# A two-layer attention hybrid on one core: the matmuls of its main part written as four 128x32 column tiles

## The chip, the cores and the metric

The kernel runs on one core of one Trainium2 chip. The metric is the time of one execution on the device, in microseconds (us). The kernel before took 1532.03 us in the median of three runs (1530.29 to 1536.46). A core has five engines with their own instruction queues: TensorE (PE, matmuls; PEld is its weight load), VectorE (DVE), ScalarE (ACT), GpSimd (POOL) and SyncE (SP), which issues the DMA transfers here.

## The reference: what is computed

The input x has two batches of 2048 tokens with 128 features, in float32. Four residual steps follow one another, each on a layer norm of x:

```
x = x + attn_a(layernorm(x))     # scores x x^T over all 2048 tokens, softmax over the first token axis
x = x + ffn(layernorm(x))        # two layers, below
x = x + attn_b(layernorm(x))     # token weights, channel weights, projection
x = x + ffn(layernorm(x))        # the same two layers once more
```

One layer of `ffn` shifts half of the features by one token, projects to queries, keys and values of 8 heads with 64 features, normalises queries and keys, turns them by a rotary table, attends within windows of 64 tokens and the window before, and projects back; then comes a gated feed-forward part:

```
q, k, v = split(shift(x) @ wqkv);  q, k = rotary(l2norm(q) * qs, l2norm(k) * ks)
x = x + local_attention(q, k, v) @ wo
h = layernorm(shift(x)) @ w1 + b1;  a, g = split(h)
x = x + (a * gelu(g)) @ w2 + b2
```

`attn_b` makes from projected queries and keys one number for each token, sends it through two short convolutions and a softmax over tokens, and multiplies the values by it and by a weight for each channel. All matmuls are in float32 but one small one for the mask.

## The kernel before

**Layout.** The state is held transposed, features on the 128 partitions, tokens along the free axis, in chunks of 512 tokens (`CH`) and blocks of 128 (`P`): 16 blocks for each batch. Matmul results go to eight PSUM banks of 128x512 (`pp` in the profile, kind `p1` in the code).

**A program written by a planner.** The functions do not issue instructions. Each calls `op(engine, cost, fn, r=..., w=..., at=..., mode=...)`, which notes an operation with its reads, writes, an assumed cost and a name. At the end `Program.run` plays all of them through a list scheduler and issues them in the order that comes out. Each operation has a place in line: its number in program order plus the offset for its name in the table `PLACES`. At each moment an engine that is free takes the ready operation with the smallest place. On TensorE `MODE` is added to the place if the operation needs another tiling of the array than the last one; on ScalarE `HOLD` is added if it needs another function table. Buffers are given out in the same pass. So the assumed costs, `PLACES`, `MODE` and `HOLD` set the order on every queue, and nothing else does: each queue then runs in that order, waiting on semaphores.

**Tilings.** TensorE's array of 128x128 can be split. `MODES = "fpsv"` are the four that the kernel before uses: `f`, the whole array; `p`, four column tiles of 128x32; `s`, 64x32 tiles, for the scores of the local attention; `v`, two column tiles of 128x64. The planner's table `SWITCH` has an assumed price for each change.

**Stages.** `first_norm` and `first_attention` do `attn_a` for the first batch (until about 130 us). The second batch's `attn_a` (`second_attention`) is done in slices beside the beginning of the main part. The main part runs 16 blocks x 2 layers x 2 batches x 2 repeats = 128 times through `Attention.block`, 32 times through `feed_forward`, and twice through `token_weights`.

**One block** on TensorE, with the lines of the profile:

- the query and key projections (L663), two operations of eight 128x32 column tiles with 256 columns each, already `p`;
- the value projection (L670), one 128x512 matmul, `f`;
- the sums for the l2 norm (L692), 128x128 by 32 columns, `f`;
- the scores (L733) with the mask added by a bfloat16 matmul (L742), 64x32 tiles, `s`;
- after exp on ScalarE, a scaling on GpSimd, a 32x32 transpose on VectorE and a round trip through DRAM buffers named `far`: the combine (L805), 16 matmuls of 128x64 with 64 columns, `v`;
- for each second block the output projection (L818), four accumulated matmuls of 128x128 by 256 columns, `f`.

`feed_forward` has six matmuls of 128 x (128, 128, 85) by 512 columns (L858) and three accumulated ones of 512 columns (L883), `f`; the means of the norms are L572 (`f`) and L553 (`p`). `second_attention` has L532 and L542 (`f`), `token_weights` L951, L1061, L1063 and some small ones (`f`). The profile shows each float32 matmul as two records of PE and two of PEld.

## Time and profile before

| | before |
|---|---|
| median of 3 runs | 1532.03 us |
| the profiled execution | 1532.57 us, its span 1530.7 us |
| mean granted TensorE clock | 0.968 |
| PE busy | 1409.7 us, 92%, 20867 matmul records |
| PEld busy | 813.8 us, 20867 records |
| DVE, ACT, POOL busy | 1219.0, 1016.3, 1070.7 us |
| chain that ended last | PE 46%, DVE 23%, DMA 10%, POOL 9%, issue 5% |
| DMA | 228.57 MB, of it 2.69 MB in the instruction queue q8 |

How to read it. The page has the busy time of each engine, then the span in 40 equal slices with a digit for the busy tenths (PEclk is the clock that TensorE was granted, in tenths). A line of a group has the line of the kernel, engine, operation, tile names as out<-in, rows*columns of the array, the moving operand, the number of records, then busy us, mean ns of one, and the idle time before with what ended it. A line of the timeline has start and length in us, then the same, with the idle time before in brackets. "issue" means that the engine waited for nothing that the profile shows. Ends of matmuls are modelled, and they overlap; the distance from the start of one operation to that of the next is the better measure.

### The profile page before, as it was taken

Reading aid. Unit: us, or ns where it says so; the run is one execution under the profiler, and the core shown is the slowest. Engines: PE = TensorE matmul, PEld = TensorE weight load, DVE = VectorE, ACT = ScalarE, POOL = GpSimd, SP = SyncE. Lnnn points to the kernel's source line nnn. Section 1 sums busy time; section 2 is a strip of 40 time slices with the busy share of each in tenths; the row PEclk is TensorE's granted clock in tenths of the full one; section 3 lists DMA queues with packets and bytes.
Section 4 is the critical chain, followed back from the end, with each engine's and each line's share of the span. In section 5 each row is a group of like instructions: output and inputs, shape, how many; then the busy total and the mean of one; then the engine's idle time right before and its main releaser. Section 6 shows DMA issues by size and latency. Waiting matters only on the chain.

```text
span 1530.7 us, 52656 instructions
## 1 busy us (share of the span) xinstructions
PE 1409.7 (92%) x20867; PEld 813.8 (53%) x20867; DVE 1219.0 (80%) x2344; ACT 1016.3 (66%) x3503; POOL 1070.7 (70%) x1308
## 2 busy tenths in 40 slices
PE   7999999999999989799999998999999998989865
PEld 4455555554555555555556554555555554655443
DVE  5366766978898989879898899689698979887761
ACT  7345675667767767657787767658576768586651
POOL 3445544857797968659797878469698869786560
PEclk9999999999999999979999999889999999999987
DMA  6441342554656554545656545535656674756441
GB/s 221 160 158 60 102 129 72 151 146 115 171 155 178 169 162 119 149 129 150 203 165 182 157 138 153 151 115 155 194 141 173 170 208 119 217 155 195 133 114 38
DMA packets 213177, 228.57 MB, mean 149 GB/s; under 512 B 40714, under 2 KB 166340, under 8 KB 212932
## 3 DMA queue, kind: packets, MB, share of 16 engines
q1 hardware_dynamic: 212932, 225.22, 51.6%
q8 instruction: 164, 2.69, 0.7%
q14 instruction: 81, 0.66, 0.1%
HBM read 126.46 MB, written 61.98 MB: 123 GB/s over the span
## 4 chain that ended last, share of the span: by engine, by line
PE 46%; DVE 23%; DMA 10%; POOL 9%; issue 5%; ACT 4%; SPq 2%; POOLq 0%; DVEq 0%; ACTq 0%
PE pp L858 7%; PE pp L663 6%; PE pp L883 4%; PE pp L805 4%; PE pp L532 4%; PE pp L516 4%; PE pp L733 3%; DVE b_n L691 3%; DMA b_c<-line 3%; DVE arena L688 3%; PE pp L542 3%; DVE arena L687 3%; PE pp L818 3%; PE pp L508 2%; PE pp L670 2%
## 5 line engine op out<-in xcount | busy, mean ns | idle before, releaser
L663 PE MATMUL pp<-wqkv,b_s 128*32 128x256 f32 x4096 | 255.3, 386 | 8.2 <-POOL b_s L609 4.6
L759 ACT ACTIVATE arena<-pp,b_m 128x96 f32<-128x96 f32 x584 | 190.3, 362 | 49.9 <-DVE b_m L754 46.5
L858 PE MATMUL pp<-b_c,w 128*128 128x512 f32 (+1 forms) x384 | 189.8, 638 | 24.5 <-POOL b_c L854 21.2
L663 PEld LDWEIGHTS pp<-wqkv,b_s 128*32 128x32 f32 x4096 | 122.5, 110 | 116.6 <-issue 27.3
L769 POOL TENSOR_TENSOR arena<-arena,b_m 128x384 f32<-128x384 f32 x146 | 118.1, 826 | 82.3 <-DVE b_m L764 72.0
L759 ACT ACTIVATE right<-pp,b_m 128x96 f32<-128x96 f32 x440 | 143.7, 366 | 37.0 <-DVE b_m L754 30.0
L701 POOL TENSOR_TENSOR arena<-arena,b_n 128x1024 f32<-128x1024 f32 x84 | 160.6, 1914 | 3.1
L733 PE MATMUL pp<-kring,b_c 64*32 64x96 f32 (+1 forms) x8448 | 132.7, 250 | 18.4 <-DVE b_c L710 11.1
L733 PEld LDWEIGHTS pp<-kring,b_c 64*32 64x32 f32 x8448 | 105.6, 107 | 73.4 <-issue 19.9
L695 POOL TENSOR_TENSOR arena<-arena 128x1024 f32<-128x1024 f32 x52 | 123.2, 2370 | 25.6 <-DVE arena L688 21.1
L754 DVE TENSOR_REDUCE b_m<-pp 128x4 f32<-128x384 f32 x256 | 130.1, 541 | 12.8 <-PE pp L742 11.7
L670 PE MATMUL pp<-wqkv,b_s 128*128 128x512 f32 x256 | 138.4, 631 | 0.0
L759 ACT ACTIVATION_READ_ACCUMULATOR arena<-pp,b_m 128x1 f32 x584 | 133.0, 229 | 0.0
L858 PEld LDWEIGHTS pp<-b_c,w 128*128 128x128 f32 (+1 forms) x384 | 68.5, 189 | 112.8 <-issue 68.1
L686 ACT ACTIVATE arena<-pp 128x512 f32<-128x512 f32 x164 | 98.1, 623 | 43.6 <-PE pp L663 40.0
L687 DVE TENSOR_TENSOR arena<-pp,b_tab 128x512 f32<-128x512 f32 x168 | 110.0, 674 | 6.9 <-ACT arena L686 3.8
L769 POOL TENSOR_TENSOR right<-right,b_m 128x384 f32<-128x384 f32 x110 | 89.1, 827 | 32.2 <-DVE b_m L764 30.3
L805 PEld LDWEIGHTS pp<-arena,b_v 128*64 128x64 f32 x2624 | 85.2, 140 | 45.0 <-issue 22.8
L805 PE MATMUL pp<-arena,b_v 128*64 128x64 f32 x2624 | 96.1, 227 | 13.1 <-DVE b_m L754 3.0
L688 DVE TENSOR_TENSOR arena<-pp,b_tab 128x512 f32<-128x512 f32 x160 | 105.0, 673 | 0.3
L759 ACT ACTIVATION_READ_ACCUMULATOR right<-pp,b_m 128x1 f32 x440 | 101.5, 233 | 0.0
L691 DVE TENSOR_REDUCE b_n<-arena 128x32 f32<-128x1024 f32 x82 | 97.7, 1194 | 0.0
(230 smaller groups left out, 3362.1 us busy)
## 6 DMA issues: line engine op xcount, KB each, us to landing
arena<-far SPq DMA_DIRECT2D x82, 512.0 KB
b_tab<-turn SPq DMA_DIRECT2D x128, 256.0 KB
b_v<-b_v SPq DMA_DIRECT2D x248, 128.0 KB
far<-arena SPq DMA_DIRECT2D x324, 96.0 KB
right<-far SPq DMA_DIRECT2D x46, 512.0 KB
far<-right SPq DMA_DIRECT2D x188, 96.0 KB
b_c<-line SPq DMA_DIRECT2D x56, 256.0 KB
turn<-b_tab SPq DMA_DIRECT2D x32, 256.0 KB
```

The costliest lines, as they stand in the source:

```text
L663: pe_.matmul(out=pq[k]()[c * 32 : c * 32 + 32, a * 256 : (a + 1) * 256], lhsT=s()[:, at : at + 32], rhs=wqkv[:, l, c * 256 : (c + 1) * 256 ...
L670: op("PE", 0.865, lambda: pe_.matmul(out=pv(), lhsT=h(), rhs=wqkv[:, l, 2 * INNER : 3 * INNER], start=True, stop=True), r=keys_of(s, q) + ...
L687: op("DVE", dve(512), lambda part3=part3, src=src, trig=trig: dv.tensor_tensor(part3(t1), src(), trig(0), ALU.mult), r=[pq[k], tab], w=[(t ...
L688: op("DVE", dve(512), lambda part3=part3, src=src, trig=trig: dv.tensor_tensor(part3(t2), src(), trig(1), ALU.mult), r=[pq[k], tab], w=[(t ...
L691: op("DVE", dve(1024), lambda: dv.tensor_reduce(nv()[:, 0:32], sq().rearrange("p (h d) -> p h d", d=32), AX.X, ALU.add), r=[sq], w=[nv], a ...
L701: lambda: po_.tensor_tensor(t1().rearrange("p (h d) -> p h d", d=32), t1().rearrange("p (h d) -> p h d", d=32), nr()[:, 0:32].unsqueeze(2) ...
L733: pe_.matmul(out=sim[par]()[a * 32 : a * 32 + 32, pair * 96 + c0 : pair * 96 + c0 + n], lhsT=qT()[rows, pair * P + a * 32 : pair * P + a * ...
L754: op("DVE", dve(384), lambda sim3=sim3, mx=mx: dv.tensor_reduce(mx(), sim3(), AX.X, ALU.max, negate=True), r=[sim[par]], w=[(nm, par)], at ...
L759: ac.activation(p()[:, hd * 96 : (hd + 1) * 96], sim[par]()[:, k * 96 : (k + 1) * 96], AF.Exp, bias=nm()[:, hd : hd + 1], accum_out=rs()[: ...
L769: lambda hs=hs: po_.tensor_tensor(p3()[:, hs, :], p3()[:, hs, :], rs()[:, hs].unsqueeze(2).to_broadcast([P, 4, 96]), ALU.mult),
L805: pe_.matmul(out=av()[par * 64 : par * 64 + 64, pair * P + w * WIN : pair * P + (w + 1) * WIN].rearrange("p (a c) -> p a c", a=2), lhsT=(v ...
L858: op("PE", pe(512), lambda: pe_.matmul(out=p_()[0:n, :], lhsT=w1[:, l, off + j * P : off + j * P + n], rhs=d(), start=True, stop=True), r= ...
```

## The change

A helper `wide(out, *parts)` writes a matmul of up to 128x128 by n columns as column tiles: the columns in pieces of 256, for each accumulated part, for each 32 rows of the output, one 128x32 matmul at `tile_position=(0, m)`. A 128x128 by 512 matmul becomes eight. All matmuls in `second_attention`, `center`, `Attention.block`, `feed_forward` and `token_weights` that used the whole array go through it and are marked `mode="p"`. The combine is written out in the same way: 32 matmuls of 128x32 with 64 columns in place of 16 of 128x64; `v` is then used by nothing. The transposes, `first_attention` and `fold_norm` stay in `f`, the scores in `s`. What is computed stays the same.

Besides, `PLACES` has new offsets throughout, `MODE` goes from 10 to 15 and `HOLD` from 20 to 50, and three assumed costs of the planner are changed; these alter the order of issue and no instruction.

```diff
 PLACES = {
-    "spread1": -71, "spread2": -145, "root1": -93, "root2": -180, "scale1": 39, "scale2": -66, "scale3": -885,
+    "spread1": -693, "spread2": -189, "root1": -243, "root2": -97, "scale1": -197, "scale2": 43, "scale3": -1790,
...
-    MODE = 10
-    HOLD = 20
+    MODE = 15
+    HOLD = 50
...
+    def wide(out, *parts, start=True, stop=True):
+
+        rows, cols = out.shape[0], out.shape[-1]
+        for c in range(0, cols, 256):
+            for k, (lhsT, rhs) in enumerate(parts):
+                for m in range(0, rows, 32):
+                    to, of = slice(m, min(m + 32, rows)), slice(c, min(c + 256, cols))
+                    pe_.matmul(
+                        out=out[to, of], lhsT=lhsT[:, to], rhs=rhs[:, of], start=start and k == 0, stop=stop and k == len(parts) - 1,
+                        tile_position=(0, m),
+                    )
...
-                for m in both:
-                    pe_.matmul(out=acc(), lhsT=xs[m](), rhs=e[m, j](), start=(m == both[0]), stop=(m == both[1]))
+                wide(acc(), *((xs[m](), e[m, j]()) for m in both))
...
-        op("ACT", act(128) + 0.1, lambda: ac.activation(r(), src(), AF.Ln, bias=eps), r=reads, w=[r], act="E", at="root1")
+        op("ACT", act(128) + 0.15, lambda: ac.activation(r(), src(), AF.Ln, bias=eps), r=reads, w=[r], act="E", at="root1")
...
-            op("PE", 0.865, lambda: pe_.matmul(out=pv(), lhsT=h(), rhs=wqkv[:, l, 2 * INNER : 3 * INNER], start=True, stop=True), r=keys_of(s, q) + [wqkv_], w=[pv], claim=[v], at="block3")
+            op("PE", 0.865, lambda: wide(pv(), (h(), wqkv[:, l, 2 * INNER : 3 * INNER])), r=keys_of(s, q) + [wqkv_], w=[pv], claim=[v], mode="p", at="block3")
...
-            op("PE", 0.15, lambda: pe_.matmul(out=pn()[:, 0:32], lhsT=twin, rhs=nv()[:, 0:32], start=True, stop=True), r=[nv, twin_], w=[pn], at="block12")
+            op("PE", 0.15, lambda: wide(pn()[:, 0:32], (twin, nv()[:, 0:32])), r=[nv, twin_], w=[pn], mode="p", at="block12")
...
-                        for par in range(2):
-                            hd, at = 2 * pair + par, (par * 4 + pair) * 32
+                        for c in range(4):
+                            hd, at = 2 * pair + c // 2, (c // 2 * 4 + pair) * 32
                             pe_.matmul(
-                                out=av()[par * 64 : par * 64 + 64, pair * P + w * WIN : pair * P + (w + 1) * WIN].rearrange("p (a c) -> p a c", a=2),
-                                lhsT=(v if w else v0)()[:, hd * DH : (hd + 1) * DH],
-                                rhs=pT().rearrange("p (a c) -> p a c", a=4)[:, 2 * w : 2 * w + 2, at : at + 32], start=True, stop=True,
+                                out=av()[c * 32 : c * 32 + 32, pair * P + w * WIN : pair * P + (w + 1) * WIN].rearrange("p (a c) -> p a c", a=2),
+                                lhsT=(v if w else v0)()[:, hd * DH + c % 2 * 32 : hd * DH + c % 2 * 32 + 32],
+                                rhs=pT().rearrange("p (a c) -> p a c", a=4)[:, 2 * w : 2 * w + 2, at : at + 32], start=True, stop=True, tile_position=(0, c * 32),
                             )
-            op("PE", 0.946, combine, mode="v", r=[pT, v, v0], w=[av], claim=[oT], at="block30")
+            op("PE", 0.94, combine, mode="p", r=[pT, v, v0], w=[av], claim=[oT], at="block30")
...
-                    for k in range(4):
-                        pe_.matmul(out=po()[:, 0:256], lhsT=wo[:, l, k, :], rhs=oT()[:, k * 256 : (k + 1) * 256], start=(k == 0), stop=(k == 3))
+                    wide(po()[:, 0:256], *((wo[:, l, k, :], oT()[:, k * 256 : (k + 1) * 256]) for k in range(4)))
...
-            op("PE", pe(512), lambda: pe_.matmul(out=p_()[0:n, :], lhsT=w1[:, l, off + j * P : off + j * P + n], rhs=d(), start=True, stop=True), r=[d, w1_], w=[p_], claim=h, at="half1")
+            op("PE", pe(512), lambda: wide(p_()[0:n, :], (w1[:, l, off + j * P : off + j * P + n], d())), r=[d, w1_], w=[p_], claim=h, mode="p", at="half1")
...
-            for j, n in enumerate(HSZ):
-                pe_.matmul(out=po(), lhsT=w2[0:n, l, j, :], rhs=h[j]()[0:n, :], start=(j == 0), stop=(j == 2))
+            wide(po(), *((w2[0:n, l, j, :], h[j]()[0:n, :]) for j, n in enumerate(HSZ)))
```

## The prediction

> **What bounds the kernel now.** I read the page first (span, busy rows, chain), then the groups of TensorE by form, then windows by stage, and last the timeline of TensorE alone, start to start.
>
> From the page of the kernel before:
>
> ```profile
> span 1530.7 us, 52656 instructions
> PE 1409.7 (92%) x20867; PEld 813.8 (53%) x20867; DVE 1219.0 (80%) x2344; ACT 1016.3 (66%) x3503; POOL 1070.7 (70%) x1308
> PEclk9999999999999999979999999889999999999987
> q8 instruction: 164, 2.69, 0.7%
> PE 46%; DVE 23%; DMA 10%; POOL 9%; issue 5%; ACT 4%; SPq 2%; POOLq 0%; DVEq 0%; ACTq 0%
> ```
>
> TensorE (PE) is the fullest engine and carries 46% of the chain; VectorE (DVE) carries 23%. The q8 row matters below: its 2.69 MB over 2 x 20867 matmuls and weight loads are 64 bytes each, and over 164 packets 16 KB each. So q8 carries TensorE's own instructions, 256 to a packet.
>
> Windows of the main part (columns: busy us and counts of PE, PEld, DVE, ACT, POOL, then clock, DMA share, GB/s):
>
> ```profile
> 130.00:330.00 200.00, 200.00 (x2479) 106.89 (x2472) 151.37 (x296) 131.70 (x462) 114.80 (x139) 1.00 0.41 114
> 330.00:1460.00 1130.00, 1048.22 (x17455) 619.18 (x17454) 981.41 (x1853) 791.32 (x2790) 876.97 (x1062) 0.97 0.57 159
> ```
>
> Up to 330 us TensorE never rests: what it saves there is saved. After that DVE is at 87% and PE at 93%, so only a part passes on.
>
> The timeline of TensorE, with a change of tiling at 706.16 and 707.24:
>
> ```profile
> 705.12 1.10 PE L670 MATMUL pp<-wqkv,b_s 128*128 128x512 f32 x2
> 706.16 1.15 PE L805 MATMUL pp<-arena,b_v 128*64 128x64 f32 x32
> 707.24 1.93 PE L663 MATMUL pp<-wqkv,b_s 128*32 128x256 f32 x32
> ```
>
> Start to start, at clock 1.00, over all operations, the common values are: a 512-column whole-array operation followed by another 0.858 us, with its successor's weights exposed 0.942 to 0.963, followed by another tiling 0.952; the column-tiled L663 0.863 (0.887 with weights exposed), 0.977 before another tiling; the 128x64 L805 0.982 and 1.082; the scores (L733 with L742) 0.879 and 1.036. Leaving a tiling thus costs 0.094 (whole), 0.114 (column), 0.100 (128x64), 0.157 (scores). Adding up distances, the 1500 us of operations are 1248 of streaming, 38 extra where the records grant half the clock (they know 1.0 and 0.5), about 90 of switches and exposed weights, 124 of waits.
>
> **The change, part by part.** Terms are TensorE time.
>
> Switches. The order has 641 changes of tiling: 239 leave whole, 173 column, 115 128x64, 114 scores: 239 x 0.094 + 173 x 0.114 + 115 x 0.100 + 114 x 0.157 = 71.6 us. In the same order after the change only the scores and a few transposes differ: 114 x (0.114 + 0.157) + 28 x 0.1 = 33.7. Saving 38.
>
> Exposed weights. Of 562 whole-after-whole operations 189 show the extra 0.084 to 0.104, together 20 us. Column tiles show 0.024, so 4.7 stay: saving 15.
>
> Streaming. Two rounds of four 256-column tiles are what L663 does: 0.863 against 0.858, on some 600 operations, +3. The norm matmul (L692, 32 columns, 128 times) takes 0.140; eight tile matmuls take at least 0.053 to stream (a quarter of L553's 0.216, whose 128 columns go the same way) and at most 0.15; I take 0.10, as L733's pairs leave 0.011 apart: -5, bounds -11 and +1. Combine (L805, 128 times) is 64 pairs instead of 32: its streaming is four times L553's 0.216, 0.86, and at the scores' 72 pairs in 0.879 it isn't held by issue; above, today's 0.982 bounds it unless 32-column loads fail to hide, which L553 excludes. I take 0.92: -8, bounds -16 and 0. Sum so far -63, bounds -50 to -75.
>
> [...]
>
> Instructions. A 512-column matmul was 2 pairs of records and becomes 16. Pairs after: L805 8192, L858 2816, L670, L818 2048 each, L883 1536, L692, L532, L542 1024 each, L572 384, L951 256, others some 300: 20,650 in place of 6,160. So 35,400 pairs, 70,700 instructions, 276 blocks of 256 instead of 163. This isn't free:
>
> ```profile
> 1144.49 0.93 PE L733 MATMUL pp<-kring,b_c 64*32 64x96 f32 x60
> ...
> 1145.34 0.88 PE L733 MATMUL pp<-kring,b_c 64*32 64x96 f32 x54
> 1147.26 0.29 PE L733 MATMUL pp<-kring,b_c 64*32 64x96 f32 x5 [1.04 <-issue]
> ...
> 1339.95 0.80 PE L805 MATMUL pp<-arena,b_v 128*64 128x64 f32 x18
> 1341.86 0.62 PE L805 MATMUL pp<-arena,b_v 128*64 128x64 f32 x14 [1.11 <-issue]
> ...
> 1362.31 0.91 PE L805 MATMUL pp<-arena,b_v 128*64 128x64 f32 x22
> 1364.59 0.51 PE L805 MATMUL pp<-arena,b_v 128*64 128x64 f32 x10 [1.37 <-issue]
> ```
>
> In the middle of an operation, where no semaphore can hold it, TensorE stops for over a microsecond. Seven such stops, some 9 us in all, fall at instruction number 193 modulo 256 of its stream (one reads 183), each ends 1.24 to 1.53 us after a q8 packet landed, and no block starts sooner than 1.24 us after its packet. Packets take 0.88 to 1.7 us and start about 1.3 us after the earlier block was begun. So a block can't be used sooner than about 1.3 + 1.05 + 1.3 = 3.6 us after the one ahead, up to 4.2. Now 6 blocks are shorter than 3.6 us, short by 7.0 us together; at 4.0 it is 9 and 10.0; this brackets the 9 seen. Scores are 144 instructions in about 0.9 us, combine becomes 128 in 0.92, all else 32 in 0.863. Cutting the order of before anew with these counts, blocks average 5.1 us; 63 of 278 fall under 3.5 us, short by 52, and 91 under 4.0, short by 89. A packet starts when, in the median, 37 instructions of the block ahead have run, and in some cases earlier, so a little lead is kept: of 52 to 89 I take 62, and +53 after today's 9. Bounds: +20 (if blocks need 3.0 us) to +100 (4.2). A stop holds all that is queued behind it on TensorE, and then who reads its banks: ScalarE waits 57.5 us for combine at L812 and 40.0 for L663 at L686 today; these grow first.
>
> [...]
>
> Order. The new places and the constants 15 and 50 alter only the order; the added 0.12 and 0.05 are the planner's, no instruction is changed by them. SP, POOL, DVE and ACT issue the same instructions and transfers; where one comes earlier on its queue, the one behind comes later. What the order can win is bounded by the 38 us of half clock below, and it can lose as much: TensorE's share of streaming was under 0.4 in nearly every 3.4 us stretch ahead of a fall of the clock, and a dense pair of operations stopped by a block, 1.8 us in 3.6, comes close to that. I take 0 (bounds -20, +20), since the two oppose each other.
>
> Sum: -63 + 53 = -10 on TensorE. In 130 to 330 us it passes whole, later at least by the 46% plus 5% of issue; I take -8. The profiled execution took 1532.6 (span 1530.7 and 1.9 around it), 0.5 above the median of 1532.03: 1524.6, so **1524** against the median.
>
> **Rivals.**
>
> Blocks stay hidden. If the new order spreads scores and combines, or a block is ready after 3.0 us, the term is +20: -43 on TensorE; if all passes on, and a tenth of the 38 us under the half clock is won, 1532 - 43 - 4 = 1485. For it: 156 of 163 blocks come unseen today, and places can move scores apart. Against: the places are given by queue costs that hold nothing of instruction blocks.
>
> Instruction blocks bind (slower). The shortage at 4.2 us is 109 on the same tally; less 9 it is +100, so +37 on TensorE; stopped stretches lower the clock, and a tenth more half clock windows cost some 4 us: 1532 + 37 x 0.7 + 4 = 1562. It decides as soon as stops exceed 72 us in all (63 saved plus 9 today), about 3.8 us for a block. Against: the lead with which half of the packets start.
>
> The others bind. DVE is busy 981 of 1130 us after 330; if it, POOL (877) and round trips through the far buffers set the pace, both the saving and the stops vanish into TensorE's 124 us of waits: only the saving to 330 us stays, about 1528. Against: PE leads the chain two to one.
>
> **How the numbers follow.** About 0.5% (7.7 us) is what a measurement of this kernel can tell from no change. My case, 1524, with its own range 1498 to 1548: 0.38, split 0.20 faster, 0.06 within, 0.12 slower. Hidden blocks, 1485: 0.23, all faster. Binding blocks, 1562: 0.29, all slower. Others bind, 1528: 0.10, 0.02 faster, 0.08 within. Together 0.45, 0.14, 0.41. Two in ten outside leaves 1478 to 1568.
>
> **What will show it.** Right: changes of tiling near 256; L670 near 0.863 start to start and without the 0.94 step; combine at 0.86 to 0.98; q8 near 276 packets, and stops "<-issue" within an operation, at one place modulo 256, adding up to about 60 us. Wrong: stops under 30 us (then 1485), or over 80, with more half clock in the PEclk row (then 1562); column tiles of L670 above 0.95, or combine above 1.0, would break the first terms; a PE row much emptier with DVE full would mean that others bind.

## The result, and the profile after

The changed kernel took 1584.35 us (median of 4 runs, 1574.25 to 1596.25) against 1531.16 of the kernel before on the same chip (4 runs, 1526.05 to 1536.46). The ratio is 1.0359, with a 95% interval of 1.0307 to 1.0412: **slower by 53 us**, where 1524 was forecast. The profiled execution took 1582.77 (span 1581.0).

The page of the changed kernel, the lines that answer to those shown of before:

```profile
span 1581.0 us, 82040 instructions
PE 1365.7 (86%) x35443; PEld 909.8 (58%) x35443; DVE 1221.8 (77%) x2344; ACT 1018.6 (64%) x3504; POOL 1072.9 (68%) x1308
PEclk9999999999999999999999999999999999999988
q8 instruction: 279, 4.57, 1.3%
PE 27%; DVE 12%; POOL 10%; DMA 8%; issue 8%; ACT 3%; SPq 2%; POOLq 0%; DVEq 0%; ACTq 0%
```

TensorE is busy 44 us less than before (1409.7) and yet the span is 50 us longer. The other engines do what they did. The instruction queue brought 279 packets where there were 164. The chain can't be set beside that of before: its shares are of the span, and here they add up to 70% only (99% before), so that the rest of the way is missing from it. Its "issue" is 8% even so, against 5%.

Its windows by stage (columns as before: busy us and counts of PE, PEld, DVE, ACT, POOL, clock, DMA share, GB/s):

```profile
130.00:330.00 200.00, 193.38 (x5036) 134.49 (x5028) 146.98 (x288) 134.69 (x472) 111.16 (x134) 1.00 0.42 110
330.00:1460.00 1130.00, 968.85 (x27758) 657.05 (x27762) 948.96 (x1790) 758.95 (x2684) 850.75 (x1033) 0.96 0.56 155
```

In the same 1130 us TensorE was busy 1048.22 before and is busy 968.85 now, and the other three do 3 to 4% less work as well (DVE 981.41 before, 948.96 now). No engine has become the bound: everything waits more.

What TensorE waited for without a semaphore, in the waits of the changed kernel (line waited for, us in total, times, longest):

```profile
PE pp L744 <- issue: 25.0, 18, 2.9
PE pp L816 <- issue: 24.4, 25, 4.2
PE pp L454 <- issue: 21.3, 14, 3.7
PE pp L753 <- issue: 4.9, 4, 1.4
PE pp L564 <- issue: 1.1, 1, 1.1
PE pp L674 <- issue: 0.5, 1, 0.5
```

The same view of the kernel before:

```profile
PE pp L733 <- issue: 3.9, 2, 2.8
PE pp L805 <- issue: 3.0, 3, 1.4
PE pp L663 <- issue: 1.3, 1, 1.3
PE pp L553 <- issue: 0.9, 1, 0.9
```

(L744 is the scores, L753 the mask, L816 the combine, L454 everything that goes through `wide`; before they were L733, L742, L805 and several lines.) Waits for instructions have gone from 9.1 us in 7 places to 77.2 in 63. In the timeline of TensorE of the changed kernel they look like this:

```profile
739.45 0.75 PE L744 MATMUL pp<-kring,b_c 64*32 64x96 f32 x39
742.51 0.46 PE L744 MATMUL pp<-kring,b_c 64*32 64x96 f32 x21 [2.31 <-issue]
...
762.57 1.93 PE L454 MATMUL pp<-b_c,w 128*32 128x256 f32 x28
768.18 2.35 PE L454 MATMUL pp<-b_c,w 128*32 128x256 f32 x18 [3.69 <-issue]
...
787.22 0.71 PE L816 MATMUL pp<-arena,b_v 128*32 128x64 f32 x33
788.67 0.59 PE L816 MATMUL pp<-arena,b_v 128*32 128x64 f32 x28 [0.74 <-issue]
```

Each splits one operation in the middle. Of the 63, 60 lie at one place of TensorE's stream: 59 at instruction 193 or 194 modulo 256, one at 200 (weight loads, matmuls and its semaphore instructions counted). They hold 73.5 us, 1.2 us each (22 in the combine, 22 in scores and mask, 14 in `wide`), and all but one end 1.1 to 1.6 us after a q8 packet landed. A wait begins only when the modelled end of the last matmul is past; counted from start to start at these places, less the usual distance, the stops hold about 90 us.

The same count in the kernel before finds five of its seven waits at that place, 5.7 us (about 7.5 from start to start). The other two, 2.8 and 0.5 us, stand in front of a whole operation and 9 to 11 us after the last packet; they are waits of another kind that the view can't name.

Who waits for them, from the waits of all engines of the changed kernel:

```profile
ACT arena L823 <- PE pp L816: 74.4, 45, 7.9
DVE b_s L834 <- PE pp L454: 53.0, 28, 8.6
ACT right L823 <- PE pp L816: 46.2, 27, 5.8
```

and the same three of the kernel before:

```profile
ACT arena L812 <- PE pp L805: 57.5, 40, 6.5
DVE b_s L824 <- PE pp L818: 23.1, 14, 8.8
ACT right L812 <- PE pp L805: 17.1, 19, 4.0
```

ScalarE's copy of the combine waits 46 us more, VectorE's sum after the out projection 30 us more.

A sum to read all the runs by: the span of TensorE is its busy time, its waits for instructions, and all its other waits. The last column is TensorE's loss by the half clock, an estimate: half of its busy time in the stretches where the records grant half (in the trace of before, a 512-column record of the whole array takes 0.429 us from start to start at full clock and 0.854 at half, a round of the column-tiled L663 0.863 and 1.707, medians); it lies inside "busy". "For instructions" is all that the waits put down to issue; in each of the runs 0 to 8 us of it lie at other places than the edge of a block. Each row is one profiled execution.

| run | span | busy | for instructions | other waits | blocks (q8) | half clock |
|---|---|---|---|---|---|---|
| before | 1530.7 | 1409.7 | 9.1 | 111.9 | 164 | 36.6 |
| after | 1581.0 | 1365.7 | 77.2 | 138.1 | 279 | 48.5 |
| after minus before | +50.3 | -44.0 | +68.1 | +26.2 | +115 | +11.9 |

More than half of the busy time saved came back as other waits, and the waits for instructions came on top. The experiments ask which part of the change did it, what limits a block, and why saved time and stopped time do not weigh the same.

### The profile page after: what moved, and what is told of

It is laid out like the page before. It is cut to its first block, busy times and chain, and to the rows that moved or that the text cites. A ratio compares the mean times of both kernels' runs of the same rounds, so it can differ in the third digit from the quotient of the medians.

```text
span 1581.0 us, 82040 instructions
## 1 busy us (share of the span) xinstructions
PE 1365.7 (86%) x35443; PEld 909.8 (58%) x35443; DVE 1221.8 (77%) x2344; ACT 1018.6 (64%) x3504; POOL 1072.9 (68%) x1308
## 4 chain that ended last, share of the span: by engine, by line
PE 27%; DVE 12%; POOL 10%; DMA 8%; issue 8%; ACT 3%; SPq 2%; POOLq 0%; DVEq 0%; ACTq 0%
PE pp L454 14%; PE pp L674 5%; PE pp L816 4%; PE pp L744 3%; DMA right<-far 2%; DMA b_c<-line 2%; POOL arena L706 2%; POOL arena L712 2%; POOL arena L780 1%; DMA arena<-far 1%; SPq L800 1%; DVE arena L698 1%; ACT arena L770 1%; DVE b_n L702 1%; DVE arena L699 1%
## 5 line engine op out<-in xcount | busy, mean ns | idle before, releaser
L454 PE MATMUL pp<-b_c,w 128*32 128x256 f32 (+2 forms) x4352 | 282.8, 392 | 36.2 <-POOL b_c L864 20.5
L674 PE MATMUL pp<-wqkv,b_s 128*32 128x256 f32 x4096 | 264.8, 391 | 6.6 <-POOL b_s L620 3.6
L770 ACT ACTIVATE arena<-pp,b_m 128x96 f32<-128x96 f32 x648 | 211.7, 359 | 43.5 <-DVE b_m L765 36.6
L454 PEld LDWEIGHTS pp<-b_c,w 128*32 128x32 f32 (+2 forms) x4352 | 154.5, 113 | 137.8 <-issue 26.2
L674 PEld LDWEIGHTS pp<-wqkv,b_s 128*32 128x32 f32 x4096 | 148.6, 113 | 74.0 <-issue 9.7
L744 PE MATMUL pp<-kring,b_c 64*32 64x96 f32 (+2 forms) x8448 | 142.8, 255 | 48.5 <-issue 25.0
L744 PEld LDWEIGHTS pp<-kring,b_c 64*32 64x32 f32 x8448 | 110.0, 109 | 94.4 <-issue 46.4
L770 ACT ACTIVATE right<-pp,b_m 128x96 f32<-128x96 f32 x376 | 122.9, 355 | 45.3 <-DVE b_m L765 30.1
L454 PE MATMUL pp<-wqkv,b_s 128*32 128x256 f32 x2048 | 138.1, 385 | 3.8 <-issue 3.4
L816 PE MATMUL pp<-arena,b_v 128*32 128x64 f32 x4864 | 93.9, 228 | 34.8 <-DMA arena<-far 19.6
L816 PEld LDWEIGHTS pp<-arena,b_v 128*32 128x32 f32 x4864 | 84.0, 115 | 49.2 <-issue 30.8
L823 ACT COPY arena<-pp 128x512 f32<-128x512 f32 x80 | 47.5, 593 | 76.5 <-PE pp L816 74.4
```

What stands on the lines that cost most here:

```text
L454: pe_.matmul(out=out[to, of], lhsT=lhsT[:, to], rhs=rhs[:, of], start=start and k == 0, stop=stop and k == len(parts) - 1, tile_position=( ...
L674: pe_.matmul(out=pq[k]()[c * 32 : c * 32 + 32, a * 256 : (a + 1) * 256], lhsT=s()[:, at : at + 32], rhs=wqkv[:, l, c * 256 : (c + 1) * 256 ...
L744: pe_.matmul(out=sim[par]()[a * 32 : a * 32 + 32, pair * 96 + c0 : pair * 96 + c0 + n], lhsT=qT()[rows, pair * P + a * 32 : pair * P + a * ...
L770: ac.activation(p()[:, hd * 96 : (hd + 1) * 96], sim[par]()[:, k * 96 : (k + 1) * 96], AF.Exp, bias=nm()[:, hd : hd + 1], accum_out=rs()[: ...
L816: pe_.matmul(out=av()[c * 32 : c * 32 + 32, pair * P + w * WIN : pair * P + (w + 1) * WIN].rearrange("p (a c) -> p a c", a=2), lhsT=(v if ...
```

## Experiments: which part of the change

The theory after the result: 256 instructions cannot follow the 256 ahead sooner than some 3.5 to 4 us (an estimate from the stops and packets of before), and the column tiles run into that. The rivals: the new order is the cause; or column tiles cost something in themselves.

**The order alone.** The kernel after, with `wide` and the combine issuing the old instructions.

```diff
-        for c in range(0, cols, 256):
+        for c in (0,):
             for k, (lhsT, rhs) in enumerate(parts):
-                for m in range(0, rows, 32):
...
+                pe_.matmul(out=out, lhsT=lhsT, rhs=rhs, start=start and k == 0, stop=stop and k == len(parts) - 1)
...
```

> The changed kernel's order of operations, unaltered, but each matmul issued as in the kernel before (whole array, combine as 128x64). Instruction blocks theory: q8 falls from 279 packets to about 165, stops at the block's edge from 83 us to under 15; changes of tiling rise from 260 to about 650 (some 38 us of TensorE); the time is near the kernel before, 1515 to 1550 us. Order theory (the new places are bad by themselves): the time stays at 1570 to 1600 us.

Measured: 1541.70 against 1531.61, ratio 1.0080 (1.0053 to 1.0106). The order by itself costs 10 us; waits for instructions are 20.3 us, 14.9 of them at the edge of a block (under 15 were expected).

**The tiles alone.** The kernel before with every call of `wide` and the combine as in the change; places, constants, modes and costs of the planner stay as they were, so the order of issue does too.

```diff
+    def wide(out, *parts, start=True, stop=True):
...
-            op("PE", 0.15, lambda: pe_.matmul(out=pn()[:, 0:32], lhsT=twin, rhs=nv()[:, 0:32], start=True, stop=True), r=[nv, twin_], w=[pn], at="block12")
+            op("PE", 0.15, lambda: wide(pn()[:, 0:32], (twin, nv()[:, 0:32])), r=[nv, twin_], w=[pn], at="block12")
...
-                        for par in range(2):
-                            hd, at = 2 * pair + par, (par * 4 + pair) * 32
+                        for c in range(4):
+                            hd, at = 2 * pair + c // 2, (c // 2 * 4 + pair) * 32
...
```

> The order of the kernel before, unaltered, but each matmul issued as the column tiles of the changed kernel. Blocks theory: some 279 packets, stops of 60 to 90 us against 63 us saved on TensorE, more time under the half clock: 1545 to 1600 us. Order theory: the tiles save their 63 us and nothing else changes, 1475 to 1510 us.

Measured: 1591.17 against 1531.61, ratio 1.0391 (1.0352 to 1.0430). From its page and its waits:

```profile
PE 1373.2 (86%) x35443; PEld 907.7 (57%) x35443; DVE 1223.4 (77%) x2344; ACT 1016.9 (64%) x3503; POOL 1074.4 (68%) x1308
q8 instruction: 278, 4.55, 1.3%
...
PE pp L816 <- issue: 34.3, 26, 3.1
PE pp L744 <- issue: 24.0, 16, 3.3
PE pp L454 <- issue: 11.0, 13, 2.6
```

The tiles do it: +59.6 us, with 80.1 us of waits for instructions. The scores' code is not touched, yet they now stop for 24.0 us: a block is short because of what stands around it. On the new order the tiles cost less (1541.70 to 1584.35, +43, medians of two separate measurements) than on the old one, so the new order is the better of the two for these tiles, and the worse for the old instructions.

**Combine as it was.** The kernel after with the combine as 128x64 matmuls again: 64 instructions in place of 128.

```diff
-                        for c in range(4):
-                            hd, at = 2 * pair + c // 2, (c // 2 * 4 + pair) * 32
+                        for par in range(2):
+                            hd, at = 2 * pair + par, (par * 4 + pair) * 32
...
-                                lhsT=(v if w else v0)()[:, hd * DH + c % 2 * 32 : hd * DH + c % 2 * 32 + 32],
+                                lhsT=(v if w else v0)()[:, hd * DH : (hd + 1) * DH],
...
```

> The changed kernel and its order, only the combine issued as 128x64 again (64 instructions in 0.98 us in place of 128 in 0.9). Blocks theory: packets to about 247, stops from 83 to about 27 us by the tally; changes of tiling from 260 to about 440, which gives 20 us back, and the combine itself some 8: 1545 to 1570 us. Order theory: only the added changes of tiling count, 1600 us or more.

Measured: 1542.69 against 1531.61, ratio 1.0056 (1.0030 to 1.0082): 42 us of the 53 are gone, and it is 2 us under the expected range. The waits of TensorE in this run:

```profile
PE pp L744 <- issue: 8.8, 10, 1.7
PE pp L816 <- issue: 8.3, 7, 3.7
PE pp L454 <- issue: 7.8, 8, 1.6
```

Blocks fall only from 279 to 246, but waits for instructions from 77.2 to 29.4: the combine, with 128 instructions in 0.89 us, uses up a block nearly as fast as the scores (144 in 0.88), and 33 packets fewer go with 48 us fewer of stops. This run against the order alone (1541.70) is also the price of all the other column tiles together: +1 us. They save 46 us of busy time, add 9 us of stops and 34 us of other waits, and win nothing.

**Column tiles of 512 columns.** The kernel after with one round of 512 columns in place of two of 256, so half the instructions in `wide`.

```diff
-        for c in range(0, cols, 256):
+        for c in range(0, cols, 512):
...
-                    to, of = slice(m, min(m + 32, rows)), slice(c, min(c + 256, cols))
+                    to, of = slice(m, min(m + 32, rows)), slice(c, min(c + 512, cols))
```

> The changed kernel with column tiles of up to 512 columns in place of 256: the same streaming with half the instructions in the 512-column operations, combine and scores as they are. Blocks theory: packets from 279 to about 243; the short blocks are those full of combines and scores, and these stay, so a tally on the order of the changed kernel at 4.0 us goes from 80 to 75 us only: 1565 to 1585 us. If instead the mean rate of instructions counts, stops fall in proportion with the packets over 163, by a third: some 28 us, 1550 us.

Measured: 1564.11 against 1531.61, ratio 1.0211 (1.0179 to 1.0242), 243 blocks, 52.1 us of waits for instructions. It lies between the two expectations, a microsecond under the lower end of the first. Nearly the same number of blocks as in the run above (243 and 246) but 21 us slower: it is not the count alone that decides, but how many instructions stand close together.

## Experiments: what limits a block

**Small matmuls at the end.** The kernel before, followed by 1024 matmuls of 8 columns that depend on nothing.

```diff
+    def small(i):
+        at = i % 4 * 32
+        pe_.matmul(out=banks[0][at : at + 32, 0:8], lhsT=meanw[:, 0:32], rhs=meanw[:, 0:8], start=True, stop=True, tile_position=(0, at))
+    for i in range(1024):
+        small(i)
```

> The kernel before with 1024 more matmuls of a 128x32 tile by 8 columns behind it: 4096 records of TensorE, 16 blocks of 256 instructions, nothing to wait for but instructions. Blocks theory: the tail runs at one block in 3.4 to 4.2 us (13 to 16 ns an instruction), in bursts with stops of 2 us and more at one place modulo 256: some 60 us for the tail. If instructions came as fast as TensorE takes them (the scores' 11 ns a pair), a block would take 1.4 us and the tail 23 us.

Measured: 1580.5 (one run) against 1530.29. The timeline of TensorE at its end:

```profile
1525.80 1.24 PE L1109 MATMUL pp<-meanw 128*32 128x8 f32 x128 [2.16 <-issue]
1529.54 1.89 PE L1109 MATMUL pp<-meanw 128*32 128x8 f32 x128 [2.50 <-issue]
1533.02 1.89 PE L1109 MATMUL pp<-meanw 128*32 128x8 f32 x128 [1.58 <-issue]
1536.49 1.89 PE L1109 MATMUL pp<-meanw 128*32 128x8 f32 x128 [1.58 <-issue]
```

Bursts of 128 matmuls with their 128 weight loads, 256 instructions, and then nothing until the next block. From 1529.54 to 1573.66 there are twelve such steps, 3.47 to 4.02 us each, **3.68 us on average**. VectorE, ScalarE and GpSimd ran nothing any more, so this is the pace of the blocks themselves. The granted clock is 0.50 from 1527.9 us on, so 1.89 us is a burst at half clock; the first one shown ran at full clock, in 1.24 us, and the next block still began 3.74 us after it. So the half clock does not set the pace. What does can be read from the q8 packets: from that first burst on, each starts 1.04 to 1.60 us after the block ahead was begun, takes 0.88 to 1.32 us, and the next block begins 1.27 to 1.59 us after it landed. No packet here started before the block ahead of it was begun.

**More instructions, nothing else.** The kernel before with L663, which was in column tiles already, cut into pieces of 64 columns: the same products in the same order of operations, with some 24,600 more instructions.

```diff
-                    for c in range(4):
+                    for p0 in range(0, 256, 64):
+                        for c in range(4):
...
-                        pe_.matmul(out=pq[k]()[c * 32 : c * 32 + 32, a * 256 : (a + 1) * 256], lhsT=s()[:, at : at + 32], rhs=wqkv[:, l, c * 256 : (c + 1) * 256], ...)
+                            pe_.matmul(out=pq[k]()[c * 32 : c * 32 + 32, a * 256 + p0 : a * 256 + p0 + 64], lhsT=s()[:, at : at + 32], rhs=wqkv[:, l, c * 256 + p0 : c * 256 + p0 + 64], ...)
```

> The kernel before with its query and key projections (L663, already column tiles) cut into pieces of 64 columns in place of 256: the same tiling, the same streaming to within 0.03 us an operation (7 us in all), 24,600 instructions more, so about 261 packets. Order, changes of tiling and the rest as before. Blocks theory: stops of 137 to 180 us by the tally, the time 1610 to 1670 us. If not the number of instructions but something else in the column tiles of the changed kernel costs (their reads, their banks): 1531 to 1545 us.

Measured: 1683.18 against 1530.29, ratio 1.0990 (1.0941 to 1.1040), with 260 blocks, fewer than the kernel after has. Of the timeline of TensorE:

```profile
623.23 1.30 PE L664 MATMUL pp<-wqkv,b_s 128*32 128x64 f32 x74
624.96 1.99 PE L664 MATMUL pp<-wqkv,b_s 128*32 128x64 f32 x128 [0.43 <-issue]
628.98 1.99 PE L664 MATMUL pp<-wqkv,b_s 128*32 128x64 f32 x128 [2.02 <-issue]
633.27 0.98 PE L664 MATMUL pp<-wqkv,b_s 128*32 128x64 f32 x54 [2.30 <-issue]
```

Four projections in a row ask for a block every 2 us and get one every 4.02 to 4.29 us, at a granted clock of 1.00. In its waits:

```profile
PE pp L664 <- issue: 101.5, 64, 3.9
```

All waits for instructions are 142.4 us, 133 more than before, and the kernel is 153 us slower (13 us more than the upper end of what was expected; the profiled execution is the slowest of four, 1693.02). Busy time rose by 55 us, of which 35 is the loss by the half clock (71.2 against 36.6); some 8 are the longer projections (0.893 us start to start at the least, against 0.863), and the rest is about what the ends of the matmuls ahead of the stops add, which count as busy. Other waits fell by 28. From start to start the stops are about 161 us here, 153 more than before. No tiling was changed, no order, and no product: that more instructions alone can slow this kernel by as much as the change did, and more, is shown by this run.

## Experiments: what saved and added time is worth

The prediction set 63 us saved against 53 us stopped as if they weighed the same. These four change TensorE's time with hardly any instructions.

**55 us less.** The third part of the feed-forward's second matmul (L883) and the fourth of the out projection (L818) are left out, in the kernel before.

```diff
-                    for k in range(4):
+                    for k in range(3):
...
-            for j, n in enumerate(HSZ):
+            for j, n in enumerate(HSZ[:2]):
...
```

> The kernel before with less work on TensorE and no other change of order: the third part of the sum in L883 and the fourth in L818 are left out, so the feed-forward part lacks its last 85 hidden features and the output projection its last 128 columns. That takes 32 x 0.86 + 64 x 0.43 = 55 us off TensorE, nearly as much as the change was to save, and no stops come with it. If TensorE's time passes on as the prediction had it (half to whole): 1477 to 1505 us. If savings hardly pass on, as the pair of runs with the order of the changed kernel suggests (46 us less busy, the same time): 1515 to 1530 us.

Measured: 1519.57 against 1530.29, ratio 0.9932 (0.9906 to 0.9959): **11 us won for 55**, as the second expectation had it. Its page, and its window after 330 us:

```profile
PE 1373.4 (90%) x20675; PEld 786.1 (52%) x20675; DVE 1220.5 (80%) x2344; ACT 1014.6 (66%) x3503; POOL 1070.5 (70%) x1308
...
330.00:1460.00 1130.00, 1017.62 (x17278) 596.21 (x17272) 981.43 (x1855) 790.88 (x2796) 876.73 (x1063) 0.96 0.58 159
```

Busy time is 36 us lower than before, though 55 us of streaming are gone: 13 us of it went to the half clock (49.8 against 36.6). Waits put down to issue rose by 9 (18.4, of them 10.3 at the edge of a block, where it was 5.7), other waits by 22.5 (134.4). In the stretch after 330 us VectorE gets as much done as before (981.43 us of work against 981.41), though TensorE is busy 31 us less there; in all, TensorE waits 50.9 us for VectorE (37.7 before), 35.7 for GpSimd (29.9) and 31.4 for transfers (23.0). Here the saving on TensorE mostly became waiting. (The profiled execution is the slowest of ten, 1528.09, and its clock the lowest of them, so the profile shows the worst case of this run.)

**55 us more.** The same two parts are added twice.

```diff
-                    for k in range(4):
+                    for j, k in enumerate((0, 1, 2, 3, 3)):
...
-            for j, n in enumerate(HSZ):
+            for k, j in enumerate((0, 1, 2, 2)):
...
```

> The mirror of the run with less work: the third part of L883 and the fourth of L818 are added a second time, so 55 us more of streaming on TensorE, with 3 whole-array matmuls' worth of instructions more at each place (some 450 records) and so no more stops; the sums hold those parts twice. If small amounts of TensorE time count alike in both directions, 0.2 to 0.35 of it: 1542 to 1552 us. If what is added counts whole, as the stops seem to: 1575 to 1590 us, and then the loss of the change is simply time added on TensorE and the gain time taken off it.

Measured: 1563.12 against 1527.82, ratio 1.0241 (1.0188 to 1.0295): +35 us, so 0.64 of the time added, between the two expectations. Other waits fall by 25 us (87.2).

**Lumps at the combine, without instructions.** In the kernel before, every third combine is preceded by matmuls whose output it overwrites.

```diff
+                for _ in range(2 if i % 3 == 0 else 0):
+                    for c in (0, 64):
+                        pe_.matmul(out=av()[c : c + 64, 0:512], lhsT=v()[:, c : c + 64], rhs=pT()[:, 0:512], start=True, stop=True)
                 for pair in range(4):
```

> The kernel before, in the same order, with every third combine (44 of 128) made longer by matmuls of 512 columns whose output the combine then overwrites: two rounds of 0.858 us, so 1.72 us in one lump, 75 us in all, and only some 700 more instructions (3 blocks). It imitates the length, the number and the place of the stops that the column tiles bring, without their instructions. All of the kernel's own work is done. If time put on TensorE in lumps at the combine passes nearly whole, as the stops seem to: 1530 + 0.8 to 1.0 x 75 = 1590 to 1605. If added time passes as the 55 us that were added to the out projection and the feed-forward did (0.64): 1578. If stops cost more than their length because TensorE stands still and the clock falls, while this keeps it streaming: 1565 to 1580.

Measured: 1578.40 against 1528.09, ratio 1.0347 (1.0310 to 1.0383), +50 us. The counts of the trace say that 48 combines, not 44, carried a lump, and a lump took 1.77 us: 85 us in all. So 0.59 of it passed: the time is that of the second expectation, and lies in the range of the third.

**The same amount in small pieces.** One round of 344 columns in each of the 128 combines.

```diff
+                for _ in range(1):
+                    for c in (0, 64):
+                        pe_.matmul(out=av()[c : c + 64, 0:344], lhsT=v()[:, c : c + 64], rhs=pT()[:, 0:344], start=True, stop=True)
                 for pair in range(4):
```

> The same amount in small pieces: each of the 128 combines made longer by one round of 344 columns, 0.576 us, 74 us in all, some 1000 more instructions (4 blocks). All of the kernel's own work is done. If the size of a lump decides (small ones vanish in TensorE's waits, as small savings do): 1545 to 1565, clearly under the run with lumps. If the place decides (the combine, for which ScalarE waits most), it comes out with the run with lumps, within 8 us. If all added time passes at 0.64: 1577, and the lumps too.

Measured: 1560.67 against 1528.09, ratio 1.0223 (1.0157 to 1.0288), +33 us. A piece took 0.629 us (0.576 was expected; what the rest is isn't shown), 80 us in all; 0.41 of it passed, as if the size of a lump decided. ScalarE's waits for the combine, first in the run with lumps:

```profile
ACT arena L815 <- PE pp L808: 95.8, 49, 6.0
ACT right L815 <- PE pp L808: 36.5, 26, 6.2
```

and in the run with small pieces:

```profile
ACT arena L815 <- PE pp L808: 86.7, 55, 4.9
ACT right L815 <- PE pp L808: 29.9, 31, 3.3
```

With 132 and 117 us ScalarE waits about as long for the combine as in the kernel after (121), and yet less passes than of the stops. So a late combine, by itself, is not what makes the stops dear. What differs is the clock: the stretches at half clock go from 99 us to 72 (lumps) and 58 (pieces), and its loss by them from 36.6 to 25.5 and 21.0. With this taken back out, the lumps passed (50 + 11) / 85 = 0.72 and the pieces (33 + 16) / 80 = 0.61, close to each other and to the 0.64 above. Streaming more is not enough for that: with the 55 us more, which lie elsewhere, the loss is 38.7. In the kernel after it went the other way (119 us at half clock, a loss of 48.5).

## Experiments: places that know of blocks

**Planned for blocks.** Column tiles of 512 columns, the combine as 128x64, and the planner counts instructions: a block may not begin sooner than 4.0 us after the last, and an operation that would stop is put back. Places were searched anew for that account, with `MODE` at 3 and `HOLD` at 0.

```diff
+    FETCH = 4.0
+    STOP = 20
+        def stop(o, t):
+            n = self.COUNT.get(o.at, 8)
+            if n < room_left:
+                return 0.0
+            return max(0.0, fetched + self.FETCH - t - o.cost * room_left / n)
...
-                return o.key + (self.MODE if self.MODES.index(o.mode) != tiling else 0)
+                return o.key + (self.MODE if self.MODES.index(o.mode) != tiling else 0) + (self.STOP * stop(o, t))
...
```

> A version meant to beat both: column tiles of 512 columns, the combine as 128x64, and a planner that counts TensorE's instructions, lets no block of 256 be used sooner than 4.0 us after the one ahead was begun, and puts operations that would stop later in line; the places are searched on that account. Blocks theory: about 210 packets, stops of 15 to 30 us; by a fifth to a third of 46 us saved, -10 to -15, against 5 to 20 us of added stops, and what the order wins: 1505 to 1530 us. If the order does not carry over to the chip: 1535 to 1555 us.

Measured: 1533.95 against 1527.82, ratio 1.0039 (1.0012 to 1.0067): no faster than before, and between the two expectations, though with column tiles this is the best of all. TensorE's sum:

```profile
PE 1361.2 (89%) x26803; PEld 714.2 (47%) x26803; DVE 1220.2 (80%) x2344; ACT 1016.0 (66%) x3504; POOL 1072.9 (70%) x1308
q8 instruction: 211, 3.46, 1.0%
```

Busy 48 us less than before, waits for instructions 18.1 (9 more), other waits 151.0 (39 more).

**The kernel before, planned for blocks.** Its instructions unchanged, with the same account and new places.

```diff
-    MODE = 10
-    HOLD = 20
+    MODE = 11
+    HOLD = 50
+    FETCH = 4.0
+    STOP = 20
...
```

> The kernel before with its instructions unchanged (no column tiles), but with places in line searched anew under an account that also counts instruction blocks (a block of 256 instructions may not come sooner than 4.0 us after the last, with 20 as the penalty of a stop). The whole of the kernel's work is done. The planner's own figure for this order is 1483 against 1512 for the order before. If places found by such an account carry over to the chip: 1505 to 1522. If the order on the chip is set by what the account doesn't hold (the run with only the order changed came out 0.8% slower, and the planned run with 512-column tiles no faster): 1525 to 1545. Stops of TensorE for instructions are expected under 15 us in all in either case, blocks near 165.

Measured: 1539.72 against 1529.39, ratio 1.0065 (1.0042 to 1.0089). The second expectation came true: what the account finds, 1483 against 1512, isn't there on the chip. Three other orders (this one, the order alone, and the one above with its column tiles) were each 0.4 to 0.8% slower than before. No run beat the kernel before with its whole work done.

All runs by the same sum (us; spans of the profiled executions):

| run | span | busy | for instructions | other waits | blocks | half clock |
|---|---|---|---|---|---|---|
| before | 1530.7 | 1409.7 | 9.1 | 111.9 | 164 | 36.6 |
| order alone | 1542.2 | 1414.2 | 20.3 | 107.7 | 165 | 37.1 |
| before, planned | 1535.0 | 1415.3 | 12.2 | 107.5 | 165 | 43.6 |
| 55 us less | 1526.2 | 1373.4 | 18.4 | 134.4 | 163 | 49.8 |
| planned for blocks | 1530.3 | 1361.2 | 18.1 | 151.0 | 211 | 36.2 |
| combine as it was | 1539.3 | 1367.8 | 29.4 | 142.1 | 246 | 35.5 |
| 512 columns | 1565.7 | 1366.9 | 52.1 | 146.7 | 243 | 56.9 |
| after | 1581.0 | 1365.7 | 77.2 | 138.1 | 279 | 48.5 |
| tiles alone | 1590.3 | 1373.2 | 80.1 | 137.0 | 278 | 52.2 |
| more instructions | 1691.0 | 1464.7 | 142.4 | 83.9 | 260 | 71.2 |
| 55 us more | 1563.8 | 1463.7 | 12.9 | 87.2 | 166 | 38.7 |
| lumps | 1577.2 | 1479.8 | 6.5 | 90.9 | 167 | 25.5 |
| small pieces | 1558.4 | 1464.3 | 8.5 | 85.6 | 168 | 21.0 |

The rows from "55 us less" to "tiles alone" have about the same busy time, 1361 to 1373, and nearly the same other waits, 134 to 151. Among them the span follows the waits for instructions: from 18 to 80 us of them it goes from 1526 and 1530 to 1590, one for one, as the sum must where its other two terms stay. Where the busy time went up instead (the last three rows and "more instructions"), other waits fell to 84 to 91.

## Why the prediction was wrong

**Switches, weights, streaming: right.** The trace after has 260 changes of tiling (256 were expected). Start to start at full clock, the column-tiled value projection takes 0.863 us (0.863 expected), the combine 0.890 to 0.897 (0.92 was taken, within 0.86 to 0.98), the norm matmul 0.060 to 0.084 (0.10 was taken). With these the sum of the savings is about 70 us instead of 63, inside its bounds of 50 to 75. Busy time shows only 44 of it. 12 us more are lost at half clock; the other 14 are about what the ends of the matmuls ahead of the stops add, which count as busy (90 us of stops from start to start against 73.5 of waits at the same place).

**The term of the blocks: right in kind, too small.** q8 has 279 packets (276 were expected). Stops were put at 62 us in all; they are 77 by the waits and about 90 from start to start. The tally of the prediction, made on the order of after with its stops taken out, is short by some 50 us at 3.6 us a block, 80 to 85 at 4.0 and 100 to 105 at 4.2. What was measured asks for 3.9 to 4.1, and the tail and the cut projection show 3.68 and 4.02 to 4.29 us directly. The step that failed here is "a little lead is kept: of 52 to 89 I take 62". The lead is gone where blocks follow each other closely, which is where they are short: in the tail each packet started 1.04 to 1.60 us after the block ahead was begun. The reading behind "the 9 seen" was off too: of the seven waits that make up 9.1 us two are not at that place and not after a packet, so that 5.7 us of waits were there before; this makes the added term 3 us larger. The run with more instructions shows how far this goes: with 260 blocks, its waits for instructions are 142.4 us.

**The step that turned the sign: "-63 + 53 = -10 on TensorE ... I take -8".** Even the measured terms, -70 and +68 (about +82 with the stops from start to start), give -2 to +12, not +53. The sum held a microsecond saved equal to a microsecond stopped. The runs show that they aren't: 55 us of streaming taken out won 11 us, the column tiles without the combine won nothing, while 133 us of waits for instructions (153 from start to start) cost 153. With a fifth of the 70 us won (14, the rate of the run with 55 us less) and the 68 us of stops at full price, the sum is +54; measured were 50 by the profiles and 53 by the medians. This sum is put together afterwards, with rates of these same runs, and so it describes the result and doesn't test it. That TensorE carried 46% of the chain and 93% of the stretch after 330 us was read as a share that passes on: "later at least by the 46% plus 5% of issue". That share did not say what a saving is worth; once TensorE is faster, the others (DVE 87% busy there) set the pace, as the rival "the others bind" said and as the longer waits for VectorE, GpSimd and transfers in the run with 55 us less show. Nor was the saving in the stretch from 130 to 330 us, which was to pass whole, kept: VectorE has done 288 instructions there against 296, and TensorE, full before, is busy 193.38 of 200. The run with the tiles alone, whose order is that of before, shows where the time goes: instruction by instruction, VectorE, ScalarE and GpSimd are 2 to 5 us behind before at 130 us, 4 to 5 at 330 us and 62 at 1460 us.

**Order 0 (bounds -20, +20): within its bounds.** It cost 10 us with the old instructions.

**The rivals.** "Instruction blocks bind", 1562, was the right mechanism, with its sign, but it too took the savings at full price (+100 - 63), so it fell 22 us short. Its point of decision, stops over 72 us in all, was passed by little (77 by the waits): by its own sum the kernel would then have been about even. It did say that stopped stretches lower the clock: 119 us at half clock against 99, and ahead of each of the 26 falls of the clock in the trace after, as of the 16 before, TensorE had streamed for under 0.4 of the last 3.4 us (counted by columns, at 0.858 us for 512). "The others bind" was right in that savings vanish in waits, and wrong in that the stops would vanish too.

**What stays open.** Why stops seem to pass on nearly whole while added streaming passes at 0.4 to 0.65 is settled only in part. The half clock explains some: its loss is 36.6 us before, 48.5 with the stops of after and 25.5 with streaming added at the combine (a difference of 23 us between after and the lumps). How a stop is counted explains more: with the 153 us from start to start, and the half clock's 35 us taken out of the cost, the run with more instructions passed on (153 - 35) / 153 = 0.77, near the 0.72 of the lumps (an estimate, from one profile each). The other way round, the run with 55 us less, with its 13 us of half clock put back, would have won (11 + 13) / 55 = 0.44. What difference is left is only argued: a wait that something else would have caused anyway can absorb an operation that streams longer ahead of time, but stops come where dense operations stand together, that is where the data is there and TensorE is behind. And each row of the table is one profile, while the runs of one kernel lie 8 to 22 us apart.

## What to carry to other kernels

Before a matmul is cut into smaller tiles, count instructions as well as streaming: look for any stretch where 256 of them would be done in under 4 us (here a block came every 3.47 to 4.02 us at the end and every 4.02 to 4.29 in the middle), and look in the waits for "issue" in the middle of an operation, even if it is only 6 us now. Don't set a saving and a loss on the fullest engine against each other one for one: take a piece of its work out and see what that is worth, which here was a fifth, and at most 0.44 with the lost clock put back. Where the order was searched with a model, a change that the model calls 2% better may come out slower, so measure the order by itself.

## What was not expected of the hardware

- TensorE's instructions came at 256 per 3.47 to 4.02 us (3.68 on average) even when the core's other engines had nothing to do (the small matmuls at the end), 4.02 to 4.29 in the middle of the kernel (the cut projections), while TensorE itself runs through 256 small ones in 1.24 us (1.89 at half clock). A packet took 0.88 to 1.32 us at the end, so most of the step isn't the transfer.
- Longer streaming at the combine came with a better granted clock: at half clock 99 us before, 72 with lumps, 58 with small pieces, and 132 where 55 us were taken out. All executions agree: their mean granted clock is 0.977 to 0.979 with lumps, 0.977 to 0.982 with pieces and 0.957 to 0.965 with 55 us less, against 0.967 to 0.974 measured beside them. With 55 us added elsewhere it stayed (0.967 to 0.974).
- Four column tiles run as fast as the whole array: 0.863 us against 0.858 for 512 columns, with 16 pairs of instructions in place of 2, and with 0.024 for exposed weights in place of 0.084 to 0.104.
